# Causal attention with a mixture of LoRA experts: a step's softmax weights summed by accumulating DMAs instead of GpSimd additions, in half-size buffers

## The chip, the cores and the metric

The kernel runs on one core of a Trainium2 chip. The metric is device time in microseconds (us) of one execution. The kernel before takes 2036.63 us, the median of three runs (2030.99 to 2042.76). The profiled execution is one more run of the same program.

Engines carry short names: PE is TensorE's matmul pipe and PEld its weight loads, DVE is VectorE, ACT is ScalarE, POOL is GpSimd, SP is SyncE, which here only issues DMAs. A name with a q (SPq, POOLq) is an engine's instruction queue.

## What is computed

Two sequences of 2048 rows with 512 features go through one pre-layernorm block, all in float32: causal attention with 16 heads of 32 features and rotary positions, and then a linear layer with eight rank-16 LoRA experts, of which each row takes the best two.

```python
x = x + _L0_attn_ref(_layernorm(x), Wq, Wk, Wv, Wo)
x = x + _L0_ffn_ref(_layernorm(x), base_w, base_b, router_w, router_b, lora_A, lora_B)

# attention, per head
scores = jnp.einsum('bhqd,bhkd->bhqk', q, k) / math.sqrt(dk)
scores = jnp.where(causal[None, None], scores, -jnp.inf)
attn = jax.nn.softmax(scores, axis=-1)
ctx = jnp.einsum('bhqk,bhkd->bhqd', attn, v)
```

What matters here is the softmax's denominator: for every query and head, the sum of the exponentials over all keys.

## The kernel before

**Tiling.** The rows are cut into eight blocks of 512 queries, four per sequence; block j of a sequence (j = 0 to 3) attends to the 512 (j + 1) keys up to its own end. The 16 heads are taken four at a time. One *step* is one block with one group of four heads, so there are 32 steps, and a step has 4 (j + 1) key tiles of 128 keys: 4, 8, 12 or 16. The last four key tiles, from `diagonal` on, lie on the causal diagonal.

**A step** has two passes. The first (`row_maxima`, L354) multiplies queries by keys (matmul at L375) and takes each row's maximum on DVE (L383, L388). The second (`attend`, L438) multiplies keys by queries (L471), adds the negated maximum by a second small matmul (L479), takes the exponential on ACT into a tile `pt` (`weigh`, L484, activation at L494), and multiplies by the values (`weighted`, L528, matmul at L539). The second pass of one step is interleaved with the first pass of the next (`side_by_side`, L611). One pass through its loop is a *phase*; a key tile takes two phases, one for each pair of heads.

**The tiles of weights.** A tile holds the weights of one key tile for four heads: 128 keys x 4 heads x 512 queries. That of key tile 0 has the tag `acc` (two buffers), all others `pt` (PTS = 3 buffers, L30 and L486). Key tiles diagonal + 1 and diagonal + 3 share one tile, since together they fit into 512 columns. On the diagonal, `affine_select` on POOL (L503) sets the masked part of two heads at a time to zero, and the multiplication by the values needs that result.

**The denominator.** `add` (L558) adds every other tile of weights into that of key tile 0, two heads at a time, on POOL (L563). It starts when key tile 0 has been multiplied by its values (`s["first"]`). When the last key tile is done, `summed` (L565) is put off by two phases (L556); it sums over the 128 keys by a matmul with ones (L568), copies the result (L574), sends four rows through DRAM to spread them over the partitions, takes reciprocals (L594), and brings them back (L597). `over_sums`, four phases after it, multiplies the step's context by them on POOL (L601).

**What sets the order.** PE, ACT and DVE run in the order in which the program is written; a planner at the end of the kernel weaves in the projections (L189, L214), the output and expert stages (L245 to L337) by their costs in us and due phases. `between` (L425) takes the multiplications by the values and `summed` from the list `due` when their phase has come; `before` (L512) takes them earlier if a new tile of weights needs their buffer. POOL and SP are not in the manual list (L65), but POOL's instructions stand in the trace in program order around the lines above. POOL also has the layernorms' small steps (L147 to L149), the rotary products (L204, L205) and a bias (L262). An engine runs its queue in order, so an instruction that waits holds up all behind it.

Of the kernel before, what the change touches and what calls it, by code (L numbers as in the profile page):

```python
# [9 lines left out]
F32 = mybir.dt.float32  # L10
BF16 = mybir.dt.bfloat16
AF = mybir.ActivationFunctionType
ALU = mybir.AluOpType
AX = mybir.AxisListType

P = 128
B, S, D = 2, 2048, 512
H, DK = 16, 32
# [3 lines left out]
BLK = 512  # L22
# [7 lines left out]
PTS = 3  # L30
# [4 lines left out]
def preln_attention_moe_lora(  # L35
# [15 lines left out]
    nc = tc.nc  # L51
# [5 lines left out]
    p2 = ctx.enter_context(tc.tile_pool(name="p2", bufs=2))  # L57
# [25 lines left out]
    ones = const.tile([P, DK], F32, name="ones")  # L83
# [337 lines left out]
    def later(phases, tile, do):  # L421
        due.append((phase[0] + phases, tile, do))
        due.sort(key=lambda entry: entry[0])
# [14 lines left out]
    def attend(s):  # L438
# [11 lines left out]
        def low(kt):  # L450
            return max(kt - diagonal, 0) * P

        def place(kt, lo=None):

            lo = low(kt) if lo is None else lo
            back = 3 * P if kt == diagonal + 3 else 0
            return slice(lo - back, BLK - back)

        def quad(*kts):

            all_of = slice(0 if len(kts) > 1 else low(kts[0]), BLK)
            sc = {}

            def take(r):
                sc[r] = bank(f"sc_{n}_{g}_{kts[0]}_{r}")

            def scores(i, r):
                if i < len(kts):
                    jj, tt = divmod(kts[i], NT)
                    rows = slice(DK * r, DK * r + DK)  # L470
                    nc.tensor.matmul(  # L471
                        out=sc[r][:, place(kts[i])], lhsT=keys[jj][rows, bass.ts(tt, P)],
                        rhs=q[rows, low(kts[i]) :], start=True, stop=False,
                    )

            def shift(i, r):
                if i < len(kts):
                    rows = slice(DK * r, DK * r + 3)
                    nc.tensor.matmul(  # L479
                        out=sc[r][:, place(kts[i])], lhsT=ones_b[rows, :],  # L480
                        rhs=s["max"][rows, low(kts[i]) :], start=False, stop=True,
                    )

            def weigh(r):  # L484
                if kts[0] not in pts:
                    tag, bufs = ("pt", PTS) if kts[0] else ("acc", 2)  # L486
                    pt = p2.tile(
                        [P, 4, BLK], F32, tag=tag, bufs=bufs, name=f"pt_{n}_{g}_{kts[0]}"
                    )
                    begun[0] += kts[0] > 0  # L490
                    for kt in kts:
                        index[kt], pts[kt] = begun[0] if kts[0] else 1 << 30, pt
                pt = pts[kts[0]]
                nc.scalar.activation(  # L494
                    pt[:, r, all_of], sc[r][:, all_of], AF.Exp, scale=1.0 / math.sqrt(DK)
                )
                if kts[0] >= diagonal and r % 2:

                    at = all_of.start
                    on = pt[:, r - 1 : r + 1, at : at + len(kts) * P]  # L500
                    if len(kts) > 1:
                        on = on.rearrange("p h (k q) -> p h k q", q=P)
                    nc.gpsimd.affine_select(  # L503
                        out=on, in_=on, compare_op=ALU.is_ge, fill=0.0, base=0,
                        pattern=[[0, 2]] + [[0, len(kts)]] * (len(kts) > 1) + [[1, P]],
                        channel_multiplier=-1,
                    )
                if kts[0] and r % 2:
                    ready.extend((kt, r - 1) for kt in kts)
                    add()  # L510

            def before():  # L512

                while kts[0] and any(tile <= begun[0] + 1 - PTS for _, tile, _ in due):
                    due.pop(0)[2](2)

            def after():
                if len(kts) == 1:
                    lo = low(kts[0])
                    mid = (lo + BLK) // 2  # L520
                    halves = [(kts[0], lo, mid), (kts[0], mid, BLK)]
                else:
                    halves = [(kt, low(kt), BLK) for kt in kts]
                later(2, index[kts[0]], lambda many: weighted(halves, many))

            return before, take, scores, shift, weigh, after

        def weighted(halves, many):  # L528

            if s["av"] is None:  # L530
                s["av"] = ps_o.tile([P, BLK], F32, tag="av", name=f"av_{n}_{g}")
            whole = len(halves) == many == 2 and halves[0][0] == halves[1][0]
            now, left = halves[:many], halves[many:]
            for kt, lo, hi in [(halves[0][0], low(halves[0][0]), BLK)] if whole else now:
                jj, tt = divmod(kt, NT)
                at = place(kt).start - low(kt)
                for r in range(4):
                    rows = slice(DK * r, DK * r + DK)
                    nc.tensor.matmul(  # L539
                        out=s["av"][rows, lo:hi],  # L540
                        lhsT=values[jj][g][:, tt, rows],
                        rhs=pts[kt][:, r, at + lo : at + hi],
                        start=(kt == 0 and lo == 0),
                        stop=(kt == tiles - 2 and hi == BLK),
                    )
            if left:
                due.insert(0, (0, index[left[0][0]], lambda many: weighted(left, many)))
                return
            kt = halves[-1][0]
            if kt == 0:  # L550
                s["first"] = True
                add()
            if kt == tiles - 2:
                s["dest"] = wide.tile([P, BLK], F32, tag="ctx", bufs=6, name=f"ctx_{n}_{g}")
                nc.scalar.copy(s["dest"], s["av"])
                later(2, 1 << 30, summed)  # L556

        def add():  # L558

            while s["first"] and ready:  # L560
                kt, r = ready.pop(0)
                some = pts[0][:, r : r + 2, low(kt) :]
                nc.gpsimd.tensor_add(some, some, pts[kt][:, r : r + 2, place(kt)])  # L563

        def summed(_):  # L565
            den = bank(f"den_{n}_{g}")
            for r in range(4):
                nc.tensor.matmul(  # L568
                    out=den[DK * r : DK * r + DK, :], lhsT=ones, rhs=pts[0][:, r, :],
                    start=True, stop=True,  # L570
                )
            if True:
                total = p2.tile([P, BLK], F32, tag="tmp", bufs=5, name=f"sum_{n}_{g}")
                nc.scalar.copy(total, den)  # L574
                if (n, g) == steps[-1]:
                    for t in range(NT):
                        some = total[:, bass.ts(t, P)]
                        nc.vector.reciprocal(some, some)
                else:


                    few = small.tile([P, 4 * BLK // P], F32, tag="few", bufs=1, name=f"few_{n}_{g}")
                    sums = dram.tile([4, BLK], F32, name=f"sums_{n}_{g}")
                    over = dram.tile([4, BLK], F32, name=f"over_{n}_{g}")
                    spread = lambda rows: rows.rearrange("r (p i) -> (r p) i", p=DK)
                    for r in range(4):
                        nc.sync.dma_start(
                            out=sums[r : r + 1, :], in_=total[DK * r : DK * r + 1, :]
                        )
                    nc.sync.dma_start(out=few, in_=spread(sums))  # L590

                def over_sums():
                    if (n, g) != steps[-1]:
                        nc.vector.reciprocal(few, few)  # L594
                        nc.sync.dma_start(out=spread(over), in_=few)
                        for r in range(4):
                            nc.sync.dma_start(  # L597
                                out=total[DK * r : DK * r + DK, :],
                                in_=over[r : r + 1, :].to_broadcast([DK, BLK]),
                            )  # L600
                    nc.gpsimd.tensor_mul(s["dest"], s["dest"], total)  # L601
                    s["ctx"].append(s["dest"])

                if (n, g) == steps[-1]:
                    over_sums()
                else:
                    set_aside(phase[0] + 4, over_sums)
# [238 lines left out]
```

## Time and profile before

| | |
|---|---|
| median of three runs | 2036.63 us |
| the profiled execution's own time | 2047.29 us |
| its span, first to last instruction | 2045.6 us |
| PE busy | 1881.6 us (92%) |
| POOL busy | 1529.8 us (75%) |
| of this the additions, L563 | 1136.8 us in 576 instructions |
| DVE, ACT busy | 1016.0 us (50%), 767.1 us (38%) |
| granted TensorE clock, mean | 0.929 |
| moved by DMA | 60.99 MB |

Busy time is added up over the instructions of an engine. The chain of work is followed back from the last instruction, at each piece to what released it; its shares say what set the end. Blocks with j = 3 end their steps 86.4 us apart on average (contexts copied from 669.55 to 1016.94 us, four steps), those with j = 2 70.8 us (386.31 to 669.55), j = 1 54.6 us (167.80 to 386.31).

### The profile page before, as it was taken

How to read it: one execution, taken by the hardware profiler on the slowest of the kernel's cores; microseconds unless marked ns; L12 is line 12 of the kernel's file. 1: busy time of each engine (PE TensorE's matmuls, PEld its weight loads, DVE VectorE, ACT ScalarE, POOL GpSimd, SP SyncE). 2: the span in 40 equal slices, each digit the busy share in tenths (PEclk: the TensorE clock that was granted, in tenths of full speed). 3: DMA queues.
4: the chain of work that ended last, by engine and by line, in shares of the span. 5: the costliest groups of instructions: out<-in, count | busy, mean ns of one | idle time of the engine just before them, and what ended most of it. 6: DMA issues, size and time to landing. Idle time of an engine off the chain costs nothing.

```text
span 2045.6 us, 31136 instructions
## 1 busy us (share of the span) xinstructions
PE 1881.6 (92%) x11840; PEld 731.9 (36%) x11840; DVE 1016.0 (50%) x2760; ACT 767.1 (38%) x1601; POOL 1529.8 (75%) x1162
## 2 busy tenths in 40 slices
PE   7898999999989999888899998999998999989778
PEld 3433433343333333333344434333433333333223
DVE  3555555555545555551255555455655455556103
ACT  1323333343523443444342334234433344335431
POOL 3657775697878887899876467668869589788992
PEclk9999999899999999798799998999999989898869
DMA  4000111001100002000010111100120000010001
GB/s 160 22 12 12 58 37 37 2 26 48 58 2 6 7 22 83 17 6 12 1 38 27 42 52 48 58 7 7 32 84 11 6 1 27 17 52 7 7 1 41
DMA packets 42254, 60.99 MB, mean 30 GB/s; under 512 B 13180, under 2 KB 13692, under 8 KB 42104
## 3 DMA queue, kind: packets, MB, share of 16 engines
q1 hardware_dynamic: 42104, 59.00, 9.4%
q8 instruction: 93, 1.52, 0.3%
q14 instruction: 57, 0.47, 0.1%
HBM read 50.08 MB, written 8.90 MB: 29 GB/s over the span
## 4 chain that ended last, share of the span: by engine, by line
PE 67%; POOL 19%; issue 8%; DVE 3%; DMA 1%; ACT 1%; SPq 0%; POOLq 0%; DVEq 0%; ACTq 0%
PE sm L375 20%; POOL pt L563 13%; PE av L539 10%; PE qps L189 5%; PE yps L328 5%; PE vps L214 5%; PE kps L189 5%; PE ops L245 5%; PE sc L479 4%; PE sc L471 2%; POOL pt L503 2%; PE den L568 2%; PE yps L335 1%; POOL k L205 1%; PE mid L273 1%
## 5 line engine op out<-in xcount | busy, mean ns | idle before, releaser
L563 POOL TENSOR_TENSOR pt<-pt,pt 128x1024 f32<-128x1024 f32 (+3 forms) x576 | 1136.8, 1990 | 173.2 <-ACT pt L494 140.3
L494 ACT ACTIVATE pt<-sc 128x512 f32<-128x512 f32 (+1 forms) x1152 | 594.2, 572 | 1006.3 <-PE sc L479 934.3
L471 PE MATMUL sc<-q,k 32*128 32x512 f32 (+3 forms) x2560 | 703.1, 618 | 14.3 <-DVE pm L383 5.4
L375 PE MATMUL sm<-k,q 32*128 32x512 f32 (+3 forms) x2560 | 655.7, 609 | 7.5 <-POOL q L205 3.6
L388 DVE TENSOR_REDUCE pm<-sm 128x1 f32<-128x512 f32 x768 | 489.8, 683 | 287.7 <-PE sm L375 262.5
L539 PE MATMUL av<-pt,v 128*32 128x512 f32 (+3 forms) x3168 | 345.6, 513 | 108.1 <-POOL pt L503 107.8
L383 DVE CUSTOM_DVE_ANT_0 sm<-sm,mask 128x128 f32<-128x128 f32 (+3 forms) x512 | 246.0, 513 | 212.3 <-PE sm L375 149.2
L375 PEld LDWEIGHTS sm<-k,q 32*128 32x128 f32 x2560 | 217.4, 197 | 328.2 <-issue 197.8
L479 PE MATMUL sc<-max,ones_b 3*128 3x512 bf16 (+3 forms) x1280 | 261.8, 365 | 0.0
L471 PEld LDWEIGHTS sc<-q,k 32*128 32x128 f32 x2560 | 236.7, 199 | 59.3 <-issue 19.9
L539 PEld LDWEIGHTS av<-pt,v 128*32 128x32 f32 x3168 | 71.5, 115 | 356.6 <-issue 171.8
L503 POOL TENSOR_SCALAR_AFFINE_SELECT pt<-pt 128x256 f32<-128x256 f32 (+1 forms) x192 | 93.1, 485 | 58.2 <-ACT pt L494 58.2
L189 PE MATMUL kps<-xnt_a,wk 128*128 128x512 f32 x256 | 121.6, 619 | 3.5 <-ACT xnt_a L160 3.4
L245 PE MATMUL ops<-wo,ctx 128*128 128x512 f32 x256 | 121.0, 618 | 3.8 <-POOL ctx L601 2.7
L189 PE MATMUL qps<-xnt_a,wq 128*128 128x512 f32 x256 | 121.5, 618 | 0.0
L479 PEld LDWEIGHTS <-ones_b 3*128 3x128 bf16 x1280 | 80.7, 99 | 107.3 <-issue 99.5
L214 PE MATMUL vps<-wv,xnt_a 128*128 128x512 f32 x256 | 117.5, 604 | 0.1
L328 PE MATMUL yps<-base_w,xnt_f 128*128 128x512 f32 x256 | 116.3, 597 | 0.0
L204 POOL TENSOR_TENSOR sw_q<-sw_q,sin 128x512 f32<-128x512 f32 x32 | 40.8, 1274 | 97.8 <-DVE sw_q L202 97.7
L204 POOL TENSOR_TENSOR sw_k<-sw_k,sin 128x512 f32<-128x512 f32 x32 | 40.7, 1272 | 54.5 <-DVE sw_k L202 39.8
L245 PEld LDWEIGHTS ops<-wo,ctx 128*128 128x128 f32 x256 | 47.3, 194 | 71.2 <-issue 62.5
L189 PEld LDWEIGHTS qps<-xnt_a,wq 128*128 128x128 f32 x256 | 47.4, 195 | 70.6 <-issue 56.9
(85 smaller groups left out, 1215.2 us busy)
## 6 DMA issues: line engine op xcount, KB each, us to landing
xa<-in_x SPq DMA_DIRECT2D x32, 256.0 KB
xf<-in_x SPq DMA_DIRECT2D x32, 256.0 KB
wo<-in_wo_t SPq DMA_DIRECT2D x8, 1024.0 KB
base_w<-in_base_wt SPq DMA_DIRECT2D x8, 1024.0 KB
out<-xf SPq DMA_DIRECT2D x32, 256.0 KB
sum<-over SPq DMA_DIRECT2D x124, 64.0 KB
cos<-in_cos SPq DMA_DIRECT2D x8, 256.0 KB
sin<-in_sin SPq DMA_DIRECT2D x8, 256.0 KB
```

The lines of the kernel that those rows point to most:

```text
L189: nc.tensor.matmul(out=pj, lhsT=w[:, c, bass.ts(g, P)], rhs=held["xn_t"][:, c, :], start=(c == 0), stop=(c == NC - 1),)
L214: nc.tensor.matmul(out=pv, lhsT=held["xn_t"][:, c, bass.ts(t, P)], rhs=wv[:, c, :], start=(c == 0), stop=(c == NC - 1),)
L245: nc.tensor.matmul(out=po, lhsT=ctx_t[c][:, bass.ts(t, P)], rhs=held["w"][:, c, :], start=(c == 0), stop=(c == NC - 1),)
L328: nc.tensor.matmul(out=po, lhsT=held["xn_t"][:, c, bass.ts(t, P)], rhs=held["w"][:, c, :], start=(c == 0), stop=False,)
L375: nc.tensor.matmul(out=sc[r][:, some[i]], lhsT=q[rows, bass.ts(ts[i], P)], rhs=keys[c][rows, : wide_of[i]], start=True, stop=True,)
L383: nc.vector.tensor_tensor_reduce(sc[r][:, here], sc[r][:, here], mask[:, BLK - w :], 1.0, 3.0 * MASKED, ALU.add, ALU.max, pm[:, t, r, c : ...
L388: nc.vector.reduce_max(pm[:, t, r, c : c + 1], sc[r], axis=AX.X)
L471: nc.tensor.matmul(out=sc[r][:, place(kts[i])], lhsT=keys[jj][rows, bass.ts(tt, P)], rhs=q[rows, low(kts[i]) :], start=True, stop=False,)
L479: nc.tensor.matmul(out=sc[r][:, place(kts[i])], lhsT=ones_b[rows, :], rhs=s["max"][rows, low(kts[i]) :], start=False, stop=True,)
L494: nc.scalar.activation(pt[:, r, all_of], sc[r][:, all_of], AF.Exp, scale=1.0 / math.sqrt(DK))
L539: nc.tensor.matmul(out=s["av"][rows, lo:hi], lhsT=values[jj][g][:, tt, rows], rhs=pts[kt][:, r, at + lo : at + hi], start=(kt == 0 and lo ...
L563: nc.gpsimd.tensor_add(some, some, pts[kt][:, r : r + 2, place(kt)])
```

## The change

`add` no longer issues an addition on POOL but a DMA from POOL's queue that adds its source to its destination (`accum_op=ALU.add`). There are as many of these as there were additions, with the same shapes: two heads each. A tile of weights now holds two heads, not four, with twice as many buffers (`pt` six, `acc` four), so a buffer comes free per pair of heads and the memory is the same. `summed` is put off by four phases, not two. All else only follows the new shapes.

```diff
             def weigh(r):
                 if kts[0] not in pts:
-                    tag, bufs = ("pt", PTS) if kts[0] else ("acc", 2)
-                    pt = p2.tile(
-                        [P, 4, BLK], F32, tag=tag, bufs=bufs, name=f"pt_{n}_{g}_{kts[0]}"
-                    )
                     begun[0] += kts[0] > 0
                     for kt in kts:
-                        index[kt], pts[kt] = begun[0] if kts[0] else 1 << 30, pt
-                pt = pts[kts[0]]
+                        index[kt], pts[kt] = begun[0] if kts[0] else 1 << 30, {}
+                if r // 2 not in pts[kts[0]]:
+
+                    tag, bufs = ("pt", 2 * PTS) if kts[0] else ("acc", 4)
+                    made = p2.tile(
+                        [P, 2, BLK], F32, tag=tag, bufs=bufs, name=f"pt_{n}_{g}_{kts[0]}_{r}"
+                    )
+                    for kt in kts:
+                        pts[kt][r // 2] = made
+                pt = pts[kts[0]][r // 2]
                 nc.scalar.activation(
-                    pt[:, r, all_of], sc[r][:, all_of], AF.Exp, scale=1.0 / math.sqrt(DK)
+                    pt[:, r % 2, all_of], sc[r][:, all_of], AF.Exp, scale=1.0 / math.sqrt(DK)
                 )
...
-                    on = pt[:, r - 1 : r + 1, at : at + len(kts) * P]
+                    on = pt[:, :, at : at + len(kts) * P]
...
                 if kts[0] and r % 2:
-                    ready.extend((kt, r - 1) for kt in kts)
+                    ready.extend((kt, r // 2) for kt in kts)
                     add()
...
-                        rhs=pts[kt][:, r, at + lo : at + hi],
+                        rhs=pts[kt][r // 2][:, r % 2, at + lo : at + hi],
...
-                later(2, 1 << 30, summed)
+                later(4, 1 << 30, summed)
 
         def add():
 
             while s["first"] and ready:
-                kt, r = ready.pop(0)
-                some = pts[0][:, r : r + 2, low(kt) :]
-                nc.gpsimd.tensor_add(some, some, pts[kt][:, r : r + 2, place(kt)])
+                kt, half = ready.pop(0)
+                nc.gpsimd.dma_start(
+                    out=pts[0][half][:, :, low(kt) :], in_=pts[kt][half][:, :, place(kt)],
+                    accum_op=ALU.add,
+                )
...
-                    out=den[DK * r : DK * r + DK, :], lhsT=ones, rhs=pts[0][:, r, :],
+                    out=den[DK * r : DK * r + DK, :], lhsT=ones, rhs=pts[0][r // 2][:, r % 2, :],
```

## The prediction

> **What bounds the kernel now.** I read the page first (busy time, then the chain), then the groups by shape, the waits, and POOL's timeline at one step's end.
>
> ```profile
> PE 1881.6 (92%) x11840; PEld 731.9 (36%) x11840; DVE 1016.0 (50%) x2760; ACT 767.1 (38%) x1601; POOL 1529.8 (75%) x1162
> PE 67%; POOL 19%; issue 8%; DVE 3%; DMA 1%; ACT 1%; SPq 0%; POOLq 0%; DVEq 0%; ACTq 0%
> PE sm L375 20%; POOL pt L563 13%; PE av L539 10%; PE qps L189 5%; PE yps L328 5%; PE vps L214 5%; PE kps L189 5%; PE ops L245 5%; PE sc L479 4%; PE sc L471 2%; POOL pt L503 2%; PE den L568 2%; PE yps L335 1%; POOL k L205 1%; PE mid L273 1%
> ```
>
> PE sets most of the end, POOL's additions (L563) 13%, or 272 us. The 8% "issue" (160 us) are largely gaps of 2.2 us between additions that run back to back, as the chain shows from 969 to 995 us and in the last step, 1922 to 1994 us, where POOL and issue make 88% of it. So where attention runs without other work beside it, POOL is the bound. The groups by shape give the price of an addition:
>
> ```profile
> L563 POOL TENSOR_TENSOR pt<-pt,pt 128x1024 f32<-128x1024 f32 x384 | 894.0, 2352 | 157.0 <-ACT pt L494 140.3 <-PE av L539 11.5
> L563 POOL TENSOR_TENSOR pt<-pt,pt 128x768 f32<-128x768 f32 x64 | 115.7, 1808 | 6.6 <-PE av L539 2.0
> L563 POOL TENSOR_TENSOR pt<-pt,pt 128x512 f32<-128x512 f32 x64 | 81.0, 1266 | 5.2
> L563 POOL TENSOR_TENSOR pt<-pt,pt 128x256 f32<-128x256 f32 x64 | 46.3, 723 | 4.4
> ```
>
> A key tile below the diagonal costs POOL 2 x 2.35 = 4.7 us. Undisturbed, PE and ACT need less: from 811.83 to 817.37 us ACT begins pairs of exponentials 1.8 to 1.95 us apart, so 3.75 us per key tile. What waits for POOL:
>
> ```profile
> PE av L539 <- POOL pt L503: 107.8, 52, 7.6
> ACT pt L494 <- POOL pt L563: 59.4, 22, 3.9
> ```
>
> PE idles 164 us in all (2045.6 - 1881.6), and 107.8 of it before the multiplication by the values of a diagonal tile, for a mask (L503) that stands in POOL's queue behind additions:
>
> ```profile
> 652.61 0.41 POOL L503 TENSOR_SCALAR_AFFINE_SELECT pt<-pt 128x256 f32<-128x256 f32 x1 [0.16 <-ACT pt L494]
> 653.10 2.35 POOL L563 TENSOR_TENSOR pt<-pt,pt 128x1024 f32<-128x1024 f32 x1
> ...
> 658.92 2.60 POOL L563 TENSOR_TENSOR pt<-pt,pt 128x768 f32<-128x768 f32 x2
> 661.48 0.64 POOL L503 TENSOR_SCALAR_AFFINE_SELECT pt<-pt 128x512 f32<-128x512 f32 x1
> 662.20 2.61 POOL L563 TENSOR_TENSOR pt<-pt,pt 128x768 f32<-128x768 f32 x2
> ...
> 666.47 0.41 POOL L503 TENSOR_SCALAR_AFFINE_SELECT pt<-pt 128x256 f32<-128x256 f32 x1
> ```
>
> The whole pattern lasts 14.3 us, from the first mask to the end of the last (652.61 to 666.88). The last price is the DMA engines'. DMA view, the first 51 us, while weights are loaded, in 40 slices:
>
> ```profile
> DMA  0599999999999999993050000004300000000000
> GB/s 0 79 374 294 286 390 397 406 389 270 316 401 367 375 390 387 387 349 122 0 175 31 0 0 0 0 0 67 141 16 0 0 0 0 0 0 0 0 0 0
> ```
>
> Full, the 16 engines copy about 390 GB/s.
>
> **What the Trainium skill says.** "DMA: Bandwidth & Descriptors", section "SWDGE vs HWDGE vs iDMA": an accumulating DMA must come from GpSimd, whose cores compute its descriptors; before has no such DMA, so no row shows it. Same page, "Rules for kernel authors": an accumulate reads its destination and writes it later, and two on the same bytes must be ordered by the first one's semaphore. So POOL waits for a landing before it can issue the next accumulate of a half. "Anatomy of one DMA — SWDGE (gpsimd) path" gives a fixed cost of some 2.0 us, and "Latency and other measured facts" about 1 us of that as descriptor work on GpSimd. Before agrees as far as it can: SP's 8 KB `over<-few`, issued at 689.71 us, has landed when SP goes on at 691.18, 1.5 us later, with next to no data.
>
> **Part by part.** *Removed*: 576 additions, 1136.8 us of POOL. POOL's counted busy time falls to 393 us.
>
> *Added*: 576 accumulates, about 1 us of POOL each (an estimate from the page). A full half is 128 x 1024 x 4 B = 524,288 B. How often those bytes cross an engine is not in the trace. One pass, as cheap as a copy: 524,288 B / 390 GB/s = 1.34 us. Two read streams (source and destination, the write beside them): 2.7 us. Three passes in turn: 4.0 us. I take two, since the read must happen twice[...]. A lone accumulate lands 2.0 + 2.7 = 4.7 us after issue. The two halves of a tile overlap, but share the engines: a round takes max(4.7, 2 x 2.7) = 5.4 us, against 4.7 us of additions. It does not matter that POOL is idle in it: the queue is in order, and the next accumulate of the half stands at its head.
>
> Where this counts: the chain has 272 + at most 160 us of additions, 432 / 4.7 = 92 rounds. 92 x 0.7 = **+64 us**.
>
> *Moved: the masks behind waits.* On the diagonal the order in POOL's queue stays, and with key tiles d+1 and d+3 sharing one tile, `ready` gives both of one half before the other half. Both add to overlapping columns, so the second waits for the first to land, nothing overlaps it, and the mask of the other half is behind it. Landing times: 768 columns 2.0 + 2.0 = 4.0 us, 256 columns 2.7, 512 columns 3.3. From the first mask: half 0 of d issued at 0.4, landed 5.1; d+1 at 5.1, landed 9.1; d+3 at 9.1, 1 us to issue; mask of half 1 ends at 10.8 (before: 9.5, that is 662.12 - 652.61); d+1 of half 1 at 10.8, landed 14.8; d+3 at 14.8, 1 us; then the masks of d+2, the last ending at 17.6 us (14.3 before). The last accumulate lands at 21 us; the last addition ended at 15.6 (668.22). PE already waits here in most steps, so the 3.3 us come on top. In the blocks with j = 0 a step's few tiles leave PE other work; I count 24 of 32 steps: 24 x 3.3 = **+80 us**.
>
> *Moved: `summed` by two phases*, 3.7 us or more, which covers most of the 5.4 us by which the sums come later. The context's multiplication has four more phases of cover and only 30.3 us of waits on its DMA now. Nothing, except at the very end.
>
> *Relief*: POOL's other work runs while accumulates fly. On the chain POOL has 19% = 389 us, of which 272 are additions and 45 masks; of the 72 others I take half: **-36 us**. It could be 0 or 72.
>
> *Half-size buffers*: a buffer comes free per pair of heads, but now at a landing. ACT's 59.4 us of waits is the whole stake, and is inside the rounds above.
>
> *Contention*: 252 MB are accumulated (384 x 524,288 B and the shorter ones), at two streams 1290 us of all engines. The small DMAs of the 31 spread denominators queue behind them: **+10 us**, an estimate from 31 times 0.33 us, one 4 KB row read in two streams at a sixteenth of 390 GB/s.
>
> Sum: 64 + 80 - 36 + 10 = +118. The profiled span becomes 2164 us; that run stands 10.7 us above the median (2047.3 to 2036.6), so about **2155 us**.
>
> **The rivals.** *Accumulating is as cheap as a copy* (one pass): a lone one lands in 3.3 us, below PE's 3.75, so the rounds give 92 x 0.95 = -87; on the diagonal the last mask ends at 14.2 us as before; relief is whole, -72. Sum -159: 1877 us. For it: the engines are nearly idle now (9.4%). Against: it reads twice. It decides once a round falls below about 4.7 us. The same side would be reached if accumulates did not wait for each other at all. *The DMA engines become the bound* (three passes, or an adder slower than the stream): a round takes 8.1 us. A j = 3 step is 12 x 8.1 + 17 for the diagonal = 114 us against 86.4, +27 each; a j = 2 step 82 against 70.8, +11; eight of each, and some 4 us per step on the diagonals of the other 16: 216 + 88 + 64 = +368, about 2400 us. For it: nothing in before shows that the adder keeps up with the stream. *Even*: relief whole and half of the masks' delay hidden by the planner's projections, with rounds of 4.9: 18 + 40 - 72 + 10, no change.
>
> **How the numbers follow.** Chances: mine 0.42 (own range 2050 to 2260), engine-bound 0.28, copy-cheap 0.20, even 0.10, of which 0.04 ends a little faster and 0.06 within 0.5%, about what a measurement of this kernel can tell from no change. So faster 0.24, same 0.06, slower 0.70. The range runs from 1965, which leaves out half of the copy-cheap case, to 2480, beyond which a slower adder would lie.
>
> **What would show it.** POOL counted busy near 393 us; DMA busy near 31% of the span if one pass, 60% if two, over 80% if three. Waits of POOL's queue for its own DMAs, 5 to 6 us per pair below the diagonal; PE's waits for L503 up from 107.8 to about 190 us; j = 3 steps 90 to 95 us apart. I am wrong if j = 3 steps come closer than 86 us, or if the waits for L503 fall: then landings are quicker than I priced, or POOL's order is another than I read.

## The result and the profile after

The changed kernel takes 2331.15 us (median; 2311.14 to 2338.72), the kernel before 2038.2 us on the same chip: 1.1426 times as long, 95% interval 1.1347 to 1.1505. The profiled execution's span is 2329.8 us against 2045.6. The direction was forecast; the size was not: 2155 us was predicted, +118 us on the span, and it became +284.

The page of the changed kernel, first the busy times and the chain:

```profile
PE 1984.0 (85%) x11888; PEld 759.7 (33%) x11888; DVE 1016.2 (44%) x2760; ACT 767.2 (33%) x1601; POOL 972.9 (42%) x1162
PE 46%; DMA 34%; POOL 8%; issue 8%; DVE 2%; ACT 1%; SPq 0%; POOLq 0%; DVEq 0%; ACTq 0%
DMA pt<-pt 31%; PE sm L375 13%; PE av L543 6%; PE qps L189 5%; PE vps L214 5%; PE ops L245 4%; PE kps L189 3%; PE yps L328 3%; POOL pt L507 3%; PE sc L479 2%; POOL pt L566 2%; PE sc L471 1%; DMA sum<-over 1%; DMA over<-few 1%; PE den L574 1%
```

DMA now holds the chain for 34% of the span, the accumulates (`pt<-pt`) alone for 31%, or 727 us, where POOL's additions held 13%. PE's own share fell from 67% to 46%. POOL's 972.9 us contain 565.7 us of DMA issuing (0.99 us each, where I had 1), without which 407 us are left (393 predicted). Two things happened to PE: it idles 346 us instead of 164 (span less busy time), +182, and it is *busy* 102 us longer, with the same work (48 multiplications by the values are split in two, which the smaller buffers and the later sum bring along at no cost, as a run below shows). The waits and the DMA issues, with the median time to landing last in a line:

```profile
POOL pt L566 <- DMA pt<-pt: 608.5, 263, 8.1
PE av L543 <- POOL pt L507: 241.8, 76, 10.9
ACT pt L498 <- DMA pt<-pt: 194.2, 65, 6.6
POOL ctx L607 <- DMA sum<-over: 89.6, 20, 10.0
...
pt<-pt POOLq DMA_DIRECT2D x384, 512.0 KB, 5.2
pt<-pt POOLq DMA_DIRECT2D x64, 384.0 KB, 4.5
pt<-pt POOLq DMA_DIRECT2D x64, 256.0 KB, 3.8
pt<-pt POOLq DMA_DIRECT2D x64, 128.0 KB, 3.2
...
q0 software_dynamic: 107520, 251.70, 61.3%
```

POOL stands 608.5 us in front of accumulates whose predecessor hasn't landed. PE waits for masks (L507 now, L503 before) 241.8 us, 134 more. The four medians lie on a line of 2.5 us and 2.7 us per 512 KB. This line does not separate a fixed part from the price of the bytes, for two reasons. The accumulates of 512 KB mostly run in pairs here, and a version further down that has them one at a time lands them in 4.6 us (median of 96). And the issue of a shorter one takes POOL 1.2 us in the lines further down, that of one of 512 KB 0.87.

One step's end, the chain of work from 915 us. Each piece of DMA is a landing waited out, and 0.5 us pass before POOL is counted as issuing the next:

```profile
915.70 5.37 DMA pt<-pt
921.07 0.02 issue
921.10 0.02 POOLq L566
921.11 0.49 issue
921.61 5.73 DMA pt<-pt
...
927.87 4.84 DMA pt<-pt
...
933.24 6.41 DMA pt<-pt
...
940.19 5.10 DMA pt<-pt
```

These five landings take 5.5 us on average, with the restart 6.0 us per key tile; additions took 4.7. The DMA view of this stretch (915.7 to 943.1 us) puts the accumulates' queue at 90.9% of all 16 engines, so the engines are nearly full there too. After it come the diagonal's masks, on POOL's timeline:

```profile
943.69 0.73 POOL L507 TENSOR_SCALAR_AFFINE_SELECT pt<-pt 128x256 f32<-128x256 f32 x1
945.82 0.87 POOL L566 DMA_DIRECT2D pt<-pt  x1 [1.40 <-DMA pt<-pt]
...
951.13 1.22 POOL L566 DMA_DIRECT2D pt<-pt  x1 [1.28 <-DMA pt<-pt]
956.03 1.20 POOL L566 DMA_DIRECT2D pt<-pt  x1 [3.68 <-DMA pt<-pt]
956.78 1.11 POOL L507 TENSOR_SCALAR_AFFINE_SELECT pt<-pt 128x512 f32<-128x512 f32 x1
...
962.92 1.20 POOL L566 DMA_DIRECT2D pt<-pt  x1 [1.59 <-DMA pt<-pt]
963.66 0.89 POOL L507 TENSOR_SCALAR_AFFINE_SELECT pt<-pt 128x256 f32<-128x256 f32 x1
```

From the first mask to the end of the last it takes 20.9 us; before, 14.3; I had worked out 17.6. Half of what I missed stands at the beginning: the diagonal's own first accumulate, at 945.82, comes 2.1 us after the first mask starts, because it too waits for a landing, that of the last key tile below the diagonal. The mask at 956.78 was held back by the accumulate at 956.03, which waited for the one of 951.13. PE's next multiplication by the values begins at 957.94, just after it, and PE has then waited 5.27 us.

### The profile page after: what moved, and what is told of

Same layout as the page of the kernel before. It is cut to its first block, busy times and chain, and to the rows that moved or that the text cites. A ratio compares the mean times of both kernels' runs of the same rounds, so it can differ in the third digit from the quotient of the medians.

```text
span 2329.8 us, 31865 instructions
## 1 busy us (share of the span) xinstructions
PE 1984.0 (85%) x11888; PEld 759.7 (33%) x11888; DVE 1016.2 (44%) x2760; ACT 767.2 (33%) x1601; POOL 972.9 (42%) x1162
## 3 DMA queue, kind: packets, MB, share of 16 engines
q0 software_dynamic: 107520, 251.70, 61.3%
## 4 chain that ended last, share of the span: by engine, by line
PE 46%; DMA 34%; POOL 8%; issue 8%; DVE 2%; ACT 1%; SPq 0%; POOLq 0%; DVEq 0%; ACTq 0%
DMA pt<-pt 31%; PE sm L375 13%; PE av L543 6%; PE qps L189 5%; PE vps L214 5%; PE ops L245 4%; PE kps L189 3%; PE yps L328 3%; POOL pt L507 3%; PE sc L479 2%; POOL pt L566 2%; PE sc L471 1%; DMA sum<-over 1%; DMA over<-few 1%; PE den L574 1%
## 5 line engine op out<-in xcount | busy, mean ns | idle before, releaser
L566 POOL DMA_DIRECT2D pt<-pt x576 | 565.7, 993 | 965.3 <-DMA pt<-pt 608.5
L471 PE MATMUL sc<-q,k 32*128 32x512 f32 (+3 forms) x2560 | 745.9, 639 | 23.5 <-ACT pt L498 11.3
L375 PE MATMUL sm<-k,q 32*128 32x512 f32 (+3 forms) x2560 | 691.3, 629 | 39.3 <-ACT pt L498 31.0
L543 PE MATMUL av<-pt,v 128*32 128x256 f32 (+3 forms) x3216 | 374.3, 543 | 243.4 <-POOL pt L507 241.8
L375 PEld LDWEIGHTS sm<-k,q 32*128 32x128 f32 x2560 | 231.4, 203 | 374.7 <-issue 214.3
L479 PE MATMUL sc<-max,ones_b 3*128 3x512 bf16 (+3 forms) x1280 | 276.3, 377 | 0.0
L471 PEld LDWEIGHTS sc<-q,k 32*128 32x128 f32 x2560 | 249.6, 205 | 76.2 <-ACT pt L498 28.7
L507 POOL TENSOR_SCALAR_AFFINE_SELECT pt<-pt 128x256 f32<-128x256 f32 (+1 forms) x192 | 146.3, 768 | 25.6 <-ACT pt L498 25.6
L245 PE MATMUL ops<-wo,ctx 128*128 128x512 f32 x256 | 131.3, 661 | 4.3 <-ACT pt L498 2.5
L607 POOL TENSOR_TENSOR ctx<-ctx,sum 128x512 f32<-128x512 f32 x32 | 44.0, 1377 | 98.9 <-DMA sum<-over 89.6
```

Source lines behind the costliest of these rows:

```text
L245: nc.tensor.matmul(out=po, lhsT=ctx_t[c][:, bass.ts(t, P)], rhs=held["w"][:, c, :], start=(c == 0), stop=(c == NC - 1),)
L375: nc.tensor.matmul(out=sc[r][:, some[i]], lhsT=q[rows, bass.ts(ts[i], P)], rhs=keys[c][rows, : wide_of[i]], start=True, stop=True,)
L471: nc.tensor.matmul(out=sc[r][:, place(kts[i])], lhsT=keys[jj][rows, bass.ts(tt, P)], rhs=q[rows, low(kts[i]) :], start=True, stop=False,)
L479: nc.tensor.matmul(out=sc[r][:, place(kts[i])], lhsT=ones_b[rows, :], rhs=s["max"][rows, low(kts[i]) :], start=False, stop=True,)
L507: nc.gpsimd.affine_select(out=on, in_=on, compare_op=ALU.is_ge, fill=0.0, base=0, pattern=[[0, 2]] + [[0, len(kts)]] * (len(kts) > 1) + [[ ...
L543: nc.tensor.matmul(out=s["av"][rows, lo:hi], lhsT=values[jj][g][:, tt, rows], rhs=pts[kt][r // 2][:, r % 2, at + lo : at + hi], start=(kt ...
```

## The experiments

All times are medians, the ratios are to the kernel before on the same chip, with 95% intervals. Theory A is that masks behind landings are most of the loss, theory B that the rounds below the diagonal are, theory C (added later) that the small transfers of the denominators are.

### One part at a time

The accumulate is taken for a part of the key tiles, a POOL addition for the others (the condition is `kt < diagonal`, `kt >= diagonal`, or never):

```diff
-                nc.gpsimd.dma_start(
-                    out=pts[0][half][:, :, low(kt) :], in_=pts[kt][half][:, :, place(kt)],
-                    accum_op=ALU.add,
-                )
+                some = pts[0][half][:, :, low(kt) :]
+                if kt < diagonal:
+                    nc.gpsimd.dma_start(
+                        out=some, in_=pts[kt][half][:, :, place(kt)], accum_op=ALU.add
+                    )
+                else:
+                    nc.gpsimd.tensor_add(some, some, pts[kt][half][:, :, place(kt)])
```

> The changed kernel, with accumulates only for key tiles below the diagonal; those on the diagonal are GpSimd additions again. Theory A: most of the loss is gone, 2038 + 64 (the prediction's term for the rounds) to 2038 + 110: 2100 to 2150 us, PE's waits for the mask near 110 us. Theory B: 2230 us or more.

Measured: 2147.23 us, ratio 1.0547 (1.0492 to 1.0601). PE's waits for masks 119.2 us.

> The changed kernel, with accumulates only on the diagonal; key tiles below it are added by GpSimd as before. Theory A: 2038 + 150 to 200, so 2190 to 2240 us, with PE's waits for the mask over 200 us. Theory B: 2040 to 2100 us.

Measured: 2185.35 us, ratio 1.0736 (1.0678 to 1.0794), 5 us below theory A's range. PE's waits for masks 209.2 us.

> The changed kernel with GpSimd additions in place of all accumulates: only the buffers of two heads and the later sum remain of the change. Theories A and B: 2025 to 2050 us, the kernel before. A third theory, that the later sum or the smaller buffers cost time by themselves: over 2080 us.

Measured: 2039.34 us, ratio 1.0007 (0.9985 to 1.0029). The buffers of two heads and the later sum cost nothing by themselves; the third theory is out.

The accumulates alone make the loss. Of 576, the 240 on the diagonal cost 150 us (ratios times 2036), the 336 below it 111, and both together 290, 29 more than the sum. Both parts are above what the prediction had for them.

### Masks ahead of the diagonal's accumulates

```diff
-                    ready.extend((kt, r // 2) for kt in kts)
+                    if kts[0] < diagonal:
+                        ready.extend((kt, r // 2) for kt in kts)
+                    else:
+                        held.extend((kt, r // 2) for kt in kts)
+                    if kts[0] == diagonal + 2 and r == 3:
+                        ready.extend(sorted(held, key=lambda e: (e[0] != diagonal, e[0])))
```

> The changed kernel, with the accumulates of the diagonal tiles held back until all masks of the step have been issued, and then issued with the two halves in turn. Theory A (the masks stand behind landings on the diagonal, and this is most of the loss): PE's waits for the mask fall from 241.8 us to under 60, the time falls by 130 to 200 us, to 2130 to 2200 us; the sum over keys may now wait some us per step for the last landings. Theory B (rounds below the diagonal are most of the loss): the waits for the mask fall, but the stall moves to buffers of weights; the time stays above 2270 us.

Measured: 2285.42 us, ratio 1.1211 (1.1154 to 1.1269). In steps that run beside a first pass, heads 2 and 3 come before 0 and 1, so the release at r == 3 missed one accumulate of 256 KB: 35 of 64 were made, 29 left out. Even so, it gained only 44 us by the ratios, and PE still waited 193.3 us for masks. The time lies in theory B's range. But this kernel moves masks past the diagonal's own accumulates alone. Those of the tiles below the diagonal still stand ahead of them, each waiting for a landing. The experiment did not take the suspected cause away, so it decides nothing between A and B; the next ones do.

### Masks off GpSimd's queue

The mask becomes a product on VectorE; `tri` is a triangle of ones and zeros, made once at the start.

```diff
-                    nc.gpsimd.affine_select(
-                        out=on, in_=on, compare_op=ALU.is_ge, fill=0.0, base=0,
-...
+                    keep = tri.unsqueeze(1)
+                    if len(kts) > 1:
+                        keep = keep.unsqueeze(1)
+                    nc.vector.tensor_mul(on, on, keep.to_broadcast(list(on.shape)))
```

> The changed kernel, with the diagonal masked on VectorE by a product with a triangle of ones and zeros instead of on GpSimd; the accumulates' order is left as it is. Theory A: PE waits for masks no longer (under 40 us instead of 241.8), and the time falls by 130 to 200 us, to 2130 to 2200 us. Theory B: the chain of landings is as long as before, the stall moves to buffers of weights and the sums over keys, and the time falls by less than 70 us.

Measured: 2141.38 us, ratio 1.0552 (1.0507 to 1.0596). PE's waits for masks are down to 7.7 us. The longest of its other waits, 33.3 us, is for a landing before the sum over keys; another 49 us it waits for exponentials on ACT, which itself waits 244.0 us for landings that free its buffers:

```profile
PE 1954.0 (91%) x11888; PEld 756.2 (35%) x11888; DVE 1117.7 (52%) x2953; ACT 768.2 (36%) x1601; POOL 879.7 (41%) x971
...
POOL pt L571 <- DMA pt<-pt: 562.7, 241, 7.5
ACT pt L504 <- DMA pt<-pt: 244.0, 82, 8.0
PE den L579 <- DMA pt<-pt: 33.3, 6, 15.3
```

POOL waits for landings almost as long as in the changed kernel (562.7 against 608.5 us), and yet 178 us are gone. POOL's waiting was not the cost; PE's work behind it was. Theory A holds, for a part that the next run sizes.

> The kernel before, with the same masks on VectorE. If GpSimd's queue held up PE by the 107.8 us that the waits show, the time falls by 60 to 110 us, to 1930 to 1980 us. If the additions themselves are the bound there, PE only waits elsewhere and it falls by less than 30 us.

Measured: 1996.36 us, ratio 0.9826 (0.9797 to 0.9855), so 35 us, between the two ranges: a third of the 107.8 us of waits. PE now waits 33.8 us for masks on VectorE. So the queue cost 178 us with accumulates and 35 with additions: 143 us of the loss are masks behind landings, or somewhat less. For VectorE's masks are not equally dear in the two kernels; here they take 1133 ns on average, beside accumulates 643:

```profile
L512 DVE TENSOR_TENSOR pt<-pt,tri 128x256 f32<-128x256 f32 (+1 forms) x192 | 217.0, 1133 | 41.9 <-ACT pt L500 39.0
L516 DVE TENSOR_TENSOR pt<-pt,tri 128x256 f32<-128x256 f32 (+1 forms) x192 | 123.3, 643 | 99.3 <-ACT pt L504 97.9
```

PE waits 26 us less for them beside accumulates (7.7 against 33.8), and how much of the 143 us is this was not tried.

> Masks on VectorE, accumulates below the diagonal, GpSimd additions on it. With masks out of the queue the accumulates of the diagonal should cost little, so nearly all of the 145 us between the kernel before and the changed one, both with masks on VectorE (1996 and 2141 us), should remain: 2110 to 2145 us. If the diagonal's landings still cost time through buffers and sums: 2040 to 2095 us.

Measured: 2073.93 us, ratio 1.0203 (1.0164 to 1.0241). The time is in the second range: with masks away, accumulates below the diagonal cost 77 us (1.0203 - 0.9826), and those on the diagonal still 71 (1.0552 - 1.0203). 77 + 71 + 143 us is the loss of 290, up to rounding, in three parts. By the profiles, the diagonal's 71 us are 34.5 us in which PE idles (183.9 against 149.4) and 36.4 us in which it is busy (1954.0 against 1917.6) at a clock of 0.912 instead of 0.929, and 1917.6 x 0.929 / 0.912 = 1953.

> The changed kernel with masks on VectorE, and on the shared diagonal tile the accumulates of the two halves in turn (d+1 of one half, d+1 of the other, d+3 of one, d+3 of the other), so that a landing is waited out beside the other half's transfer. If the 67 us that the diagonal's accumulates cost without masks behind them come from landings that nothing overlaps, two of them per step (3 to 4.5 us each) are now shared: 2141 falls by 30 to 70 us, and PE's 33.3 us of waits in front of the sum over keys shrink. If they come from the transfers themselves or from buffers freed later, it falls by less than 15 us.

```diff
-                    ready.extend((kt, r // 2) for kt in kts)
+                    held.extend((kt, r // 2) for kt in kts)
+                    if len(kts) == 1 or len(held) == 4:
+                        ready.extend(sorted(held, key=lambda e: e[0]))
+                        held.clear()
```

Measured: 2142.71 us, ratio 1.0518 (1.0463 to 1.0573): no difference that can be told from none. The 71 us of the diagonal do not come from two landings in a row that nothing overlaps. PE's waits in front of the sum over keys are 35.0 us here, and ACT's for buffers that a landing frees 246.5. The first is about as large as the idle part of the 71 us, but no run took it away; which of the two, or what else, makes the 71 us stays open.

### The small transfers

```diff
-                    few = small.tile([P, 4 * BLK // P], F32, tag="few", bufs=1, name=f"few_{n}_{g}")
-...
+                for t in range(NT):
+                    some = total[:, bass.ts(t, P)]
+                    nc.vector.reciprocal(some, some)
```

> The changed kernel, with the denominators' reciprocals taken where they lie, on VectorE, as the last step already does it, so that the small transfers through DRAM go and GpSimd's product no longer waits for them. Theory C (the small transfers queue behind the accumulates, GpSimd's product waits for them at the head of its queue, and all accumulates behind it wait too): GpSimd's 89.6 us of waits for them go, the time falls by 40 to 90 us, to 2240 to 2290 us. Theories A and B: less than 25 us, since VectorE has some 3 us more per step and no one waits for it.

Measured: 2318.89 us, ratio 1.1412 (1.1373 to 1.1451). POOL's 89.6 us of waits are gone with the transfers, the time is not; the interval covers the changed kernel's ratio. Theory C falls as a large cause: POOL now waits 308.1 us for exponentials instead of 227.7. VectorE is busy 95 us longer with the reciprocals; a gain of some us that this hides is not excluded.

### What the sums cost at all

> The changed kernel with no summing of weights at all (576 accumulates left out, so the denominators hold key tile 0 alone and the output is not the reference's). It shows what the sums cost in either kernel. If GpSimd's additions were the bound of before where attention ran alone, 1880 to 1930 us; if they were mostly hidden, 1980 us or more. PE's waits for the mask should all but vanish, under 30 us.

```diff
-                kt, half = ready.pop(0)
-                nc.gpsimd.dma_start(
-...
+                ready.pop(0)
```

Measured: 1837.88 us, ratio 0.9058 (0.9014 to 0.9101).

```profile
PE 1792.6 (97%) x11888; PEld 714.5 (39%) x11888; DVE 1013.6 (55%) x2760; ACT 766.4 (41%) x1601; POOL 404.4 (22%) x586
core 0: 1850.4 us, clock 0.982
```

This kernel leaves out the sums. Additions cost 9.4% of the time before, more than I took them to (1880 to 1930 us); the accumulates cost 24%. And PE is busy 89 us less than before with the same work, at a clock of 0.982 instead of 0.929.

### The clock

PE's busy time times its granted clock is nearly the same in all kernels (those that the table leaves out give 1743 to 1781):

| kernel | PE idle, us | clock | PE busy, us | busy x clock |
|---|---|---|---|---|
| no sums | 57.8 | 0.982 | 1792.6 | 1760 |
| before, masks on VectorE | 123.4 | 0.948 | 1869.2 | 1772 |
| before | 164.0 | 0.929 | 1881.6 | 1748 |
| changed, masks on VectorE | 183.9 | 0.912 | 1954.0 | 1782 |
| accumulates below the diagonal only | 218.1 | 0.913 | 1930.4 | 1762 |
| accumulates on the diagonal only | 275.3 | 0.904 | 1908.2 | 1725 |
| changed | 345.8 | 0.874 | 1984.0 | 1734 |

So the 102 us come with the clock: 1881.6 x 0.929 / 0.874 = 2000 us, against 1984 measured. The clock falls with idle time, but in these rows accumulates mostly rise with it. To part the two, the kernel before was made to wait without any:

```diff
+                    for _ in range(3):
                         nc.gpsimd.affine_select(
```

> The kernel before, with every mask on GpSimd executed three times in a row (the second and third change nothing), 186 us more of GpSimd's time, no accumulate anywhere. It makes PE wait as in the changed kernel, without DMA. If TensorE's granted clock falls because PE waits, PE's busy time times the clock stays near 1750 us, as in all runs so far: with some 250 us idle the clock is near 0.90 and PE is busy some 1930 us. If it falls because of the accumulates' traffic, the clock stays at 0.93 and PE's busy time at 1880 us.

Measured: 2193.77 us, ratio 1.079 (1.0753 to 1.0828).

```profile
core 0: 2195.0 us, clock 0.898
...
PE av L540 <- POOL pt L504: 225.2, 70, 9.5
```

PE is busy 1914.0 us and idles 281.0; 1914.0 x 0.898 = 1719. The clock falls where PE waits, with no accumulate in the kernel, and by about as much as in the row of the table with as much idle time. A single stall shows it too. Here PE waits from 635.15 to 642.80 us; the clock is 1.00 from 633 to 635, 0.50 from 637 to 645, and 1.00 again from 647. The changed kernel's end of a step, with stalls of 6.36 and 5.27 us, has a mean clock of 0.58 (the last figures are clock, DMA share and GB/s):

```profile
943.70:964.50 20.80, 11.95 (x86) 4.67 (x86) 5.09 (x22) 3.15 (x9) 11.06 (x14) 0.58 0.82 139
```

After the second of these stalls, PE works from 957.94 on, but the clock stays at 0.50 until about 969. The Trainium skill describes this fall: "TensorE: Matmul & The Clock Gate", section "Part 1: The HAM clock gate", has activity release a throttle that is otherwise on, and idle windows of about 3.4 us bring it back. The stalls above agree that waiting brings the clock down, to 0.50, but not on the length: it fell 1.4 us after PE had stopped in the one with masks thrice, and 2.9 us after in the stall of 5.27 us. The idle time alone does not fix the clock, however: with masks on VectorE, the changed kernel has 0.912 at 183.9 us, and accumulates below the diagonal only, with masks on GpSimd, 0.913 at 218.1.

### A version that beats both

One half of every second key tile below the diagonal is an accumulate. In the tiles between, half 0 is added before half 1, so that two additions pass before the accumulate must have landed; the lines for this order and for the masks on VectorE are left out here.

```diff
+                some = pts[0][half][:, :, low(kt) :]
+                if kt < diagonal and kt % 2 and half:
+                    nc.gpsimd.dma_start(
+                        out=some, in_=pts[kt][half][:, :, place(kt)], accum_op=ALU.add
+                    )
+                else:
+                    nc.gpsimd.tensor_add(some, some, pts[kt][half][:, :, place(kt)])
```

> A version meant to beat both: the changed kernel's buffers, masks on VectorE, and one accumulate for every second key tile below the diagonal (half 1 of odd tiles); the other three halves of each two tiles, and the diagonal, are GpSimd additions, ordered so that the accumulate has a tile's time to land. GpSimd then has 3 x 2.35 + 0.86 = 7.9 us per two key tiles instead of 9.4. If the sums' pace sets the end where attention runs alone, 0.75 us less on 92 to 111 tiles: 1910 to 1930 us. If the landings come through all the same, or GpSimd's queue is held up elsewhere: 1985 us or more.

Measured: 1980.94 us, ratio 0.9737 (0.9697 to 0.9777), between the two ranges. It is the fastest that computes everything, 0.9 points below the kernel before with masks on VectorE (0.9826, and the intervals do not touch). POOL's timeline shows what was wanted, an accumulate that takes POOL 0.85 us where an addition takes 2.35, and the accumulates land one at a time in 4.6 us (median):

```profile
867.90 2.35 POOL L584 TENSOR_TENSOR pt<-pt,pt 128x1024 f32<-128x1024 f32 x1
870.20 0.85 POOL L580 DMA_DIRECT2D pt<-pt  x1
870.80 2.62 POOL L584 TENSOR_TENSOR pt<-pt,pt 128x1024 f32<-128x1024 f32 x1
...
pt<-pt POOLq DMA_DIRECT2D x96, 512.0 KB, 4.6
```

But 18 us came of it, not 70. POOL still waits 68.4 us for landings and 90.3 for masks on VectorE; how much of the missing gain is theirs was not tried.

## Why the prediction was wrong

The path was right: rounds that wait for landings, and masks behind them that PE needs. The sum was too small, 118 us where the span grew by 284. Its terms are times in which PE waits, so they are compared with PE's idle time here, from five kernels: those with masks on VectorE (accumulates nowhere, below the diagonal only, everywhere), the one before and the changed one:

| term | predicted, us | idle time of PE, us | whole cost, us |
|---|---|---|---|
| rounds, relief, contention | 38 | 26.0 | 77 |
| masks | 80 | 121.3 | 143 |
| later sums | 0 | 34.5 | 71 |
| all | 118 | 181.8 | 290 |

Of the 166 us that are missing, 102 are busy time of PE at a lower clock. That is the step that failed most: a microsecond in which PE waits was priced at one microsecond. The masks, 41 us too small, and the sums, 34.5 us put at nothing, are the other two.

**What held.** The price of a lone accumulate: 4.7 us predicted, 4.6 us measured in the version with one at a time. Its fixed part came from the Trainium skill, "DMA: Bandwidth & Descriptors", section "Anatomy of one DMA — SWDGE (gpsimd) path", and that measurement agrees with it. The DMA engines' work, 1290 us predicted for two streams and 61.3% of the span, or 1428 us, measured, which fits neither one pass nor three. GpSimd's issue of 1 us (0.99). That masks would stand behind landings, and that PE would pay for it. That the smaller buffers cost nothing.

**The rounds, +64 - 36 + 10 = +38.** Measured without masks in the way: 77 us. The two halves together land in 5.5 us on average, as priced (5.4), but 0.5 us pass between a landing and the next issue, so that a round takes 6.0 us. With this the sum would be 92 x 1.3 = 120 us, less 36 us of relief: 84, close to 77. That is luck, for only 26 us of the 77 are idle time of PE (149.4 against 123.4 us), less than the 38 predicted; the rest is busy time, with a clock of 0.929 instead of 0.948. How large the relief was is not shown. The 10 us of contention with small transfers are not there: removing these changed nothing that can be told. Steps with j = 3 now end 101.6 us apart (755.30 to 1161.85 us, four steps), where 90 to 95 was expected; before it was 86.8 (347.39 us for the four steps, not the 86.4 each that is given at the beginning).

**The masks, +80.** Measured: 143. The step that failed here is "24 x 3.3 us", in both factors. The pattern of a step's end takes 20.9 us in the step shown, not 17.6: the diagonal's first accumulate, taken to go out 0.4 us after the first mask starts, goes out after 2.1 us, behind a landing from below the diagonal; the two of 384 KB on the path take 4.6 and 4.4 us, not 4.0; and 0.3 to 0.5 us pass at each restart. And I let the blocks with j = 0 off: the accumulates on the diagonal alone (expected to cost nothing there) moved the end of the first four steps from 167.80 to 184.05 us.

**`summed` moved by two phases, "Nothing".** Wrong. Accumulates on the diagonal cost 71 us even with masks out of the queue. PE waits 33.3 us before the sum over keys there, and is busy 36.4 us longer at the lower clock; that this wait makes the loss is not shown.

**What was missing.** I added up stalls one for one: a microsecond in which PE waits was to cost a microsecond. It costs more, since the clock falls with it. +182 us of idle time came with +102 us of busy time, 1.56 us for each. This price is not a constant: 1.28 in the kernel with masks thrice (+117.0 us idle, +32.4 busy), 1.84 between no sums and before, 2.86 for the accumulates below the diagonal with masks on VectorE (+26.0, +48.4). At 1.28 to 1.56, my +118 would have become some 151 to 184 by this alone. It was to be seen before: the kernel before shows a clock of 0.929, and 0.70 in its last step (1922.40 to 1993.60 us), where PE is busy 57.67 of 71.20 us.

**The rivals.** "The DMA engines become the bound", 2400 us, was closer in time, but for another reason: its three passes did not come, and a round of 8.1 us neither. The engines do stand near their limit where attention runs alone, at two streams. "As cheap as a copy" is refuted: a lone accumulate of 512 KB lands in 4.6 us, not 3.3.

## What to carry to other kernels

Replacing an engine's work by a transfer which the same engine must wait for frees the engine on paper only: ask what else is in its queue, and who waits for that. Here about half of the loss lay neither in the sums nor in the engine that made them, but in small masks that had shared its queue with much less harm as long as the work ahead of them was short. And when a change makes TensorE wait, price each microsecond above one: look at the clock that the profile shows in and after the stalls that are there already.

## What the runs showed of the hardware

An accumulate of 512 KB from SBUF to SBUF lands 4.6 us after its issue when there is one at a time, and 5.2 us after it (median) when most run in pairs; those of 128, 256 and 384 KB take 3.2, 3.8 and 4.5 us. Its issue costs GpSimd 0.85 us for 512 KB and 1.2 us for the shorter ones in the step shown, and the next one that depends on it is counted as issued 0.3 to 0.5 us after the landing.

A mask's record on GpSimd is 768 ns long on average, 485 without accumulates. In the step shown this is overlap with the issue ahead of it: the mask at 956.78 is 0.47 us longer than the same mask before (1.11 against 0.64), and the issue at 956.03 ends 0.45 us after it begins. So it does not show that GpSimd computes more slowly beside an accumulate.

TensorE's mean granted clock went from 0.982 to 0.874 as its idle time went from 58 to 346 us, with busy time times clock between 1719 and 1782 us throughout, and it fell in a kernel without accumulates as well. In single stalls of 5.27 and 7.65 us it fell from 1.00 to 0.50, 2.9 and 1.4 us after PE had stopped, and after PE had resumed it stayed there for about 11 us in the one and 4 us in the other.
